# Two products of a chunked recurrence split into two halves of 64 channels

## The chip, the cores and the metric

The kernel runs on one core of a Trainium2 chip. A core has a matrix engine (TensorE, PE in the profile, with its weight loads listed as PEld), a vector engine (DVE), a scalar engine (ACT), GpSimd (POOL) and a queue engine (SP) that here starts all the DMAs. The metric is the device time of one execution in microseconds. Three runs of the kernel before took 1005.9, 1007.14 and 1010.24 us: the median is 1007.14 us.

## What is computed

The input x is 16 sequences of 128 tokens with 512 channels. A first layer is an RWKV block: layer norm, five mixed projections (k, w, v, r, g), a linear recurrence over the tokens in 32 heads of 16 channels, a group norm, a gate, an output projection and a gated feed-forward. A second layer is an attention of x over a context. The part that matters here is the recurrence. For each head, with a state s of 16 by 16:

```python
def step(s, rkvw):
    r_t, k_t, v_t, w_t = rkvw
    a = k_t[..., :, None] * v_t[..., None, :]
    out = jnp.einsum('bhi,bhij->bhj', r_t, u * a + s)
    s = a + w_t[..., :, None] * s
    return (s, out)
```

Written out, the output of token t is the sum over earlier tokens s of the scalar "r_t times all decays between times k_s" times v_s, plus a term with u for s = t, plus r_t times the decayed starting state.

## The kernel before

All arithmetic is float32. The 16 sequences are worked in 8 groups g of n = 2 sequences b. Each group passes through stages: stageB and stageB2 (norm, mixing, projections), stageR (the recurrence), stageC (output projection and feed-forward), stageL (attention), with stageE and stageX making and loading the context's tensors. A step of the outer loop holds different stages of different groups (OFF, ORDER, DLY); `interleave` advances them piece by piece, at their `yield`s, and so several independent streams of work lie in each engine's program at the same time. The order of the instructions in each engine's queue is then chosen by the framework's own scheduler, which places an instruction when its inputs and its buffer are expected to be ready. On the chip, every engine takes its queue in that order.

Channels lie on partitions in stageR: 512 channels are 4 blocks `cc` of 128 partitions, each block 8 heads of 16 channels. The 128 tokens are cut into 4 chunks c of 32. Three products on TensorE belong together:

- The level products (L433 to L453). Inside a chunk, pairs of tokens at distances of 4, 8 and 16 are done level by level (LEV). A copy of k, `ks`, is spread by 8 DMAs into `KX` (`expand`, L402 to L410): for each block KX has 8 slots, one for each head, and head h fills only its own 16 partitions of slot h; all else stays zero from the start. A product of r (32 tokens of one chunk as weights, 128 channels deep) with KX (16 tokens for 8 heads, 128 columns) gives the pair values of all 8 heads at once, since the zeros keep the heads apart (L441). The four chunks write four different groups of 32 partitions of one PSUM bank `pl`, one bank for each sequence. Then `copy_predicated` on DVE moves the valid ones into `AM` (L445).
- The states at chunk starts (L468 to L504). `pu` holds the products of k and v of a chunk (L489): weights of 32 tokens by 64 channels, so two chunks (different rows of TensorE) and two halves of the channels (different columns) take four parts of the array; chunk 2 is done by itself. DVE decays the state of each chunk (`Sn`, L497), adds `pu` (L498), and `spread` (L474) writes it with zeros between the heads (mask `bdm`) into `Sx`, 8 slots of 16 columns for each chunk and block.
- The output `po` (L513 to L524). For each block, four products of r (128 channels deep) with Sx (L517, 128 columns), and eight products of the transposed AM with v (L522, 64 columns) that add to the same PSUM bank. ACT copies `po` to `y` (L526).

PSUM buffers are taken in turn by tag. `pq`, `p4`, `pl`, `pk`, `pu`, `pa` and `po` all share the tag "lv", which has two banks: each new one waits until the last but one is read out.

A float32 matmul in this kernel shows as two weight loads and two matmul instructions; a transpose as one of each. The profile writes a matmul's place as rows*columns of the array: `128*32` is 128 rows by 32 columns, `32*64` is 32 rows by 64 columns.

Of the kernel before, what the change touches and what calls it, by code (L numbers as in the profile page):

```python
# [7 lines left out]
FP = mybir.dt.float32  # L8
# [3 lines left out]
ALU = mybir.AluOpType  # L12
# [6 lines left out]
n = 2  # L19
# [15 lines left out]
def rwkv_xattn_kernel(ctx: ExitStack, tc: tile.TileContext, a: dict, out: bass.AP):  # L35
    nc = tc.nc
    const = ctx.enter_context(tc.tile_pool(name="const", bufs=1))
    small = ctx.enter_context(tc.tile_pool(name="small", bufs=4))
    ps = ctx.enter_context(tc.tile_pool(name="ps", bufs=1, space=bass.MemoryType.PSUM))
    dr = ctx.enter_context(tc.tile_pool(name="dr", bufs=2, space=bass.MemoryType.DRAM))  # L40
    sb = ctx.enter_context(tc.tile_pool(name="sb", bufs=2))
    sb1 = ctx.enter_context(tc.tile_pool(name="sb1", bufs=1))
# [31 lines left out]
    st = load("st", [128, 2, 4, B])  # L74
    w1 = load("maa_w1", [128, 4, 160])

    LATE = dict(td_w1=[128, 4, 64], td_w2=[128, 512], l1w=[128, 4, 128], l1b=[128, 4], emat=[128, 32], bdm=[128, 8, 16],
                lvm=[128, 3, 16], dgm=[128, 32])
    late = {k: const.tile(v, I32 if k in ("lvm", "dgm") else FP, name=k) for k, v in LATE.items()}
    td1, td2, l1w, l1b, emat, bdm, lvm, dgm = late.values()  # L80
# [20 lines left out]
    stk = [const.tile([98, 5, 256], FPR, name=f"sk{i}") for i in range(2)]  # L101


    KX = const.tile([128, 4 * n, 8, 64], FP, name="KX")
# [248 lines left out]
    def stageR(g):  # L353
        d = D[g]
        k, r, w, vt = d["k"], d["r"], d["w"], d["vt"]

        wl = sb1.tile([128, 4 * n, 124], FP, name="wl")
        src = w.rearrange("p c b t -> p (c b) t")
        for m in PRO:
# [42 lines left out]
        def expand(li):  # L402

            m = LEV[li]
            ks = sb1.tile([128, 4 * n, 64], FP, name="ks", tag="sq")
            nc.scalar.copy(ks.rearrange("p a (q m) -> p a q m", m=m),
                           kf.rearrange("p a (q s m) -> p a q s m", s=2, m=m)[:, :, :, 0])
            for h in range(8):
                p = slice(16 * h, 16 * h + 16)
                nc.sync.dma_start(out=KX[p, :, h], in_=ks[p])  # L410

        def wblock(m, half):
            if m == 1:
# [17 lines left out]
        decay(rf, 2, 1)  # L431
        yield
        for li, m in enumerate(LEV):  # L433
            pl = []
            for b in range(n):
                t = ps.tile([128, 512], FP, name="pl", **T("lv"))
                pl.append(t)
                for cc in range(4):
                    for c in range(4):
                        cs = slice(32 * c, 32 * c + 32)  # L440
                        nc.tensor.matmul(t[cs, 128 * cc : 128 * cc + 128], lhsT=r[:, cc, b, cs],  # L441
                                         rhs=KX[:, n * cc + b, :, 16 * c : 16 * c + 16], start=True, stop=True)
            yield
            for b in range(n):
                nc.vector.copy_predicated(  # L445
                    AM[:, b].rearrange("p h (q s m) -> p h q s m", s=2, m=m)[:, :, :, 0],
                    lvm[:, li].rearrange("p (q m) -> p q m", m=m)[:, None].to_broadcast([128, 32, 16 // m, m]),
                    pl[b].rearrange("p (h q m) -> p h q m", h=32, m=m))
            decay(rf, m, 1)
            if li < 2:  # L450
                expand(li + 1)
                decay(kf, 2 * m, 0)
            yield  # L453
        y = sb1.tile([128, n, 512], FP, name="y")
        var = small.tile([128, n, 32], FP, name="var", bufs=2)
        for b in range(n):

            for q in range(4):
                nc.sync.dma_start(out=VX[32 * q : 32 * q + 32, :, q],
                                  in_=d["vD"][:, b, 128 * q : 128 * q + 128].rearrange("(c s) f -> s c f", s=32))  # L460
# [7 lines left out]
            Sx = sb1.tile([128, 4, 4, 8, 16], FP, name="Sx")  # L468
            Sc = s0[:, b, :, None, :].to_broadcast([128, 4, 4, 16])

            def spread(c, src):

                o = Sx[:, c].rearrange("p m (a q) j -> p m a (q j)", a=2)
                nc.vector.tensor_tensor(o, src, bdm.rearrange("p (a q) j -> p a (q j)", a=2)[:, None].to_broadcast([128, 4, 2, 64]), ALU.mult)  # L474

            nc.vector.tensor_tensor(Sx[:, 0], s0[:, b, :, None, :].to_broadcast([128, 4, 8, 16]),
                                    bdm[:, None].to_broadcast([128, 4, 8, 16]), ALU.mult)
            vb = vt[:, b].rearrange("p (q x j) -> p x q j", q=4, x=8)
            yield

            pu = [ps.tile([128, 4, 4, 16], FP, name="pu", **T("lv")) for _ in range(2)]

            def gains(cs_):
                for cc in range(4):
                    for hf in range(2):
                        f = slice(64 * hf, 64 * hf + 64)
                        for c in cs_:
                            cs = slice(32 * c, 32 * c + 32)
                            nc.tensor.matmul(pu[c][f, cc], lhsT=kt[cs, 128 * cc + 64 * hf : 128 * cc + 64 * hf + 64],  # L489
                                             rhs=vb[cs, 2 * cc + hf], start=True, stop=True)  # L490

            gains((0, 1))
            yield
            for c in range(3):
                wc = wl.rearrange("p (c b) s -> p c b s", b=n)[:, :, b, WOFF[32] + c]
                Sn = sb.tile([128, 4, 4, 16], FP, name="Sn")
                nc.vector.tensor_tensor(Sn, Sc, wc[:, :, None, None].to_broadcast([128, 4, 4, 16]), ALU.mult)  # L497
                nc.vector.tensor_tensor(Sn, Sn, pu[c], ALU.add)  # L498
# [4 lines left out]
                Sc = Sn  # L503
                yield  # L504

            at = sb1.tile([128, 8, 128], FP, name="at")
            for x4 in range(2):
                pa = ps.tile([128, 4, 128], FP, name="pa", **T("lv"))
                for x in range(4):
                    nc.tensor.transpose(pa[:, x], AM[:, b, 4 * (4 * x4 + x) : 4 * (4 * x4 + x) + 4].rearrange("p h s -> p (h s)"), ident)  # L510
                nc.scalar.copy(at[:, 4 * x4 : 4 * x4 + 4], pa)
            yield
            po = ps.tile([128, 512], FP, name="po", **T("lv"))  # L513
            for cc in range(4):
                for c in range(4):
                    cs = slice(32 * c, 32 * c + 32)
                    nc.tensor.matmul(po[cs, 128 * cc : 128 * cc + 128], lhsT=r[:, cc, b, cs],  # L517
                                     rhs=Sx[:, c, cc].rearrange("p h j -> p (h j)"), start=True, stop=True)
                for x in (2 * cc, 2 * cc + 1):
                    for c in range(4):  # L520
                        cs = slice(32 * c, 32 * c + 32)
                        nc.tensor.matmul(po[cs, 64 * x : 64 * x + 64], lhsT=at[:, x, cs],  # L522
                                         rhs=VX[:, c, :, 16 * x : 16 * x + 16], start=False, stop=True,
                                         skip_group_check=True)  # L524
            yield
            nc.scalar.copy(y[:, b], po)  # L526
# [226 lines left out]
def _prep(np, inp):  # L753

    f = lambda nm: np.asarray(inp[nm])
# [12 lines left out]
    r = {}  # L768
# [18 lines left out]
    s0 = ctx[:, 2:18].reshape(G, n, 4, 8, 16, 16)  # L787
# [6 lines left out]
    r["bdm"] = np.repeat(r["emat"][:, 0:8, None], 16, 2)  # L794
    t = p % 32
    q = np.arange(16)
    lv = []
    for m in LEV:
        s = q // m * 2 * m + q % m
# [23 lines left out]
```

## Time and profile before

| | |
|---|---|
| median of three runs | 1007.14 us |
| the profiled execution's own time | 1012.07 us |
| its span from first to last instruction | 1010.3 us |
| mean granted clock of TensorE | 0.973 |
| TensorE busy | 919.9 us (91%) |
| DVE busy | 648.3 us (64%) |
| ACT busy | 495.6 us (49%) |
| level products (L441) | 1536 instructions, busy 52.3 us |
| state products (L517) | 512 instructions, busy 29.0 us |

Busy time is the time in which at least one instruction of the group was under way, so instructions that overlap count once. A mean duration is that of one instruction from start to modelled end; where four instructions run at the same time in four parts of the array, the group's time is far below their number times the mean. The chain of waits is the list of work, followed back from the last instruction, that sets the end; its pieces follow one another in time without overlap, so the time of a piece of TensorE work divided by its instructions says how fast the engine got through them. The 40 slices show the busy share over the span, 25 us each.

### The profile page before, as it was taken

The page shows a single profiled execution, that of the slowest core. Times are in us where ns is not written, and L with a number is a line of the kernel's source. Part 1 is how long each engine was busy: PE and PEld are TensorE (multiplying, and loading weights), DVE is VectorE, ACT ScalarE, POOL GpSimd, SP SyncE. Part 2 cuts the span into 40 slices and gives each one's busy share as a digit, 9 for nine tenths or more (in the row PEclk, how much of TensorE's full clock was granted, in tenths as well). Part 3 has the DMA queues.
Part 4 walks back from the last instruction along what each step waited for, and adds up shares of the span by engine and source line. Part 5 has one row for each costly group of instructions (what it writes and reads, how often), then busy time and mean ns, then how long its engine had stood idle before and what let it go on. Part 6 is the DMA issues. An engine that isn't in the chain of part 4 may idle for free.

```text
span 1010.3 us, 19691 instructions
## 1 busy us (share of the span) xinstructions
PE 919.9 (91%) x7780; PEld 632.1 (63%) x7780; DVE 648.3 (64%) x1609; ACT 495.6 (49%) x1049; POOL 60.3 (6%) x92
## 2 busy tenths in 40 slices
PE   3799999898999899999989999999999997997965
PEld 2576867565566776586757666676757555754643
DVE  7767787874694778667945785597746754543231
ACT  3555273353343754644545553365535454546343
POOL 6201010000000000000000000000000000000000
PEclk9799999999899999999999999999999998999997
DMA  6755647357324245453345334624344433333200
GB/s 169 237 188 181 198 162 255 82 160 217 100 63 127 88 136 153 132 182 112 95 108 176 108 101 118 178 77 158 84 120 155 144 80 91 95 94 94 83 22 21
DMA packets 76461, 129.93 MB, mean 129 GB/s; under 512 B 33697, under 2 KB 43425, under 8 KB 76368
## 3 DMA queue, kind: packets, MB, share of 16 engines
q1 hardware_dynamic: 76370, 128.68, 42.1%
q8 instruction: 61, 1.00, 0.4%
q14 instruction: 30, 0.25, 0.1%
HBM read 100.32 MB, written 22.04 MB: 121 GB/s over the span
## 4 chain that ended last, share of the span: by engine, by line
PE 67%; DVE 11%; DMA 10%; ACT 7%; SPq 2%; issue 2%; POOL 0%; DVEq 0%; ACTq 0%; POOLq 0%
PE ptk L576 16%; PE pj L219 11%; PE pj L603 5%; PE pv L326 5%; PE pO L702 5%; PE pS L688 4%; PE pl L441 4%; PE pA L697 2%; DMA out_dram<-x 2%; SPq L410 2%; PE po L517 1%; PE po L522 1%; PE p L240 1%; PE pu L489 1%; DMA x<-in_x_dram 1%
## 5 line engine op out<-in xcount | busy, mean ns | idle before, releaser
L219 PE MATMUL pj<-xm,wb 128*128 128x256 f32 x768 | 181.5, 387 | 7.0 <-DMA wb<-in_Wk_dram 3.5
L219 PEld LDWEIGHTS pj<-xm,wb 128*128 128x128 f32 x768 | 143.9, 193 | 37.6 <-issue 8.5
L138 POOL TENSOR_TENSOR rs<-rs,mhalf 128x1 f32<-128x1 f32 x64 | 43.1, 680 | 752.9 <-DVE rs L123 681.8
L702 PEld LDWEIGHTS pO<-AT,MV 128*128 128x128 f32 x448 | 59.1, 198 | 22.3 <-ACT AT L699 10.3
L692 ACT ACTIVATE e<-pS,nm 128x512 f32<-128x512 f32 x64 | 44.4, 695 | 52.6 <-DVE nm L690 52.6
L702 PE MATMUL pO<-AT,MV 128*128 128x128 f32 x448 | 63.6, 286 | 6.3 <-ACT AT L699 6.3
L690 DVE TENSOR_REDUCE nm<-pS 128x1 f32<-128x512 f32 x64 | 43.7, 687 | 38.6 <-PE pS L688 38.6
L688 PE MATMUL pS<-MV,Mn 128*128 128x512 f32 x112 | 60.6, 624 | 6.6 <-DMA MV<-mvD 5.5
L576 PE MATMUL ptk<-wb,kk 128*128 128x512 f32 x128 | 60.5, 617 | 5.8 <-DMA wb<-in_Wfv_dram 5.7
L286 DVE TENSOR_TENSOR xm<-px,sx 128x512 f32<-128x512 f32 x80 | 53.9, 685 | 18.2 <-PE px L283 18.0
L694 ACT ACTIVATE e<-e,nm 128x512 f32<-128x512 f32 x64 | 46.1, 726 | 33.4 <-DVE nm L693 33.3
L699 ACT COPY AT<-pA 128x512 f32<-128x512 f32 x64 | 37.6, 587 | 48.9 <-PE pA L697 43.3
L576 PE MATMUL ptk<-wb,sx 128*128 128x512 f32 x128 | 58.4, 598 | 1.1 <-DMA wb<-in_Wfr_dram 1.1
L326 PE MATMUL pv<-wb,xm 128*128 128x512 f32 x128 | 58.6, 603 | 0.6 <-DVE xm L286 0.6
L603 PE MATMUL pj<-xk,wb 128*128 128x256 f32 x256 | 58.4, 382 | 0.2 <-DVE xk L145 0.2
L576 PE MATMUL ptk<-wb,yT 128*128 128x512 f32 x128 | 58.0, 602 | 0.0
L703 DVE SCALAR_TENSOR_TENSOR x<-pO,cb,x 128x128 f32<-128x128 f32 x64 | 22.2, 348 | 51.5 <-PE pO L702 51.3
L441 PE MATMUL pl<-KX,r 128*32 128x128 f32 x1536 | 52.3, 275 | 2.6 <-DMA KX<-ks 2.6
L287 DVE TENSOR_TENSOR xm<-xm,xaT 128x512 f32<-128x512 f32 x80 | 54.2, 684 | 0.3
L603 PEld LDWEIGHTS pj<-xk,wb 128*128 128x128 f32 x256 | 47.5, 190 | 7.8 <-ACT AT L699 0.8
L697 PE MATMUL pA<-ident,e 128*128 128x128 f32 x256 | 41.8, 288 | 11.3 <-ACT e L694 9.7
L697 PEld LDWEIGHTS pA<-ident,e 128*128 128x128 f32 x256 | 30.7, 146 | 33.4 <-ACT e L694 16.1
(162 smaller groups left out, 1684.2 us busy)
## 6 DMA issues: line engine op xcount, KB each, us to landing
mvD<-MVe SPq DMA_DIRECT2D x16, 512.0 KB, 5.3
wb<-in_Wk_dram SPq DMA_DIRECT2D x16, 512.0 KB, 3.8
wb<-in_Wr_dram SPq DMA_DIRECT2D x16, 512.0 KB, 3.7
wb<-wvc SPq DMA_DIRECT2D x16, 512.0 KB, 3.5
wb<-in_Wg_dram SPq DMA_DIRECT2D x16, 512.0 KB, 4.7
wb<-in_Wo_dram SPq DMA_DIRECT2D x16, 512.0 KB, 3.6
wb<-in_Wfk_dram SPq DMA_DIRECT2D x16, 512.0 KB, 4.2
wb<-in_Wfr_dram SPq DMA_DIRECT2D x16, 512.0 KB, 3.7
```

The lines of the kernel that those rows point to most:

```text
L219: nc.tensor.matmul(pj[:, m], lhsT=wb[:, m, cc, :], rhs=xm[:, cc], start=cc == 0, stop=cc == 3)
L286: nc.vector.tensor_tensor(xm[:, sl], px.rearrange("p c (b t) -> p c b t", b=n), sx[:, sl], ALU.mult)
L287: nc.vector.tensor_tensor(xm[:, sl], xm[:, sl], xaT[:, sl, :, 1:129], ALU.add)
L326: nc.tensor.matmul(pv, lhsT=xm[:, m, b], rhs=wbs[m // 2][:, m % 2], start=m == 0, stop=m == 3)
L441: nc.tensor.matmul(t[cs, 128 * cc : 128 * cc + 128], lhsT=r[:, cc, b, cs], rhs=KX[:, n * cc + b, :, 16 * c : 16 * c + 16], start=True, sto ...
L576: nc.tensor.matmul(pt, lhsT=act[:, m, b], rhs=wbs[m // 2][:, m % 2], start=m == 0, stop=m == 3)
L603: nc.tensor.matmul(pj[:, m], lhsT=wb[:, m, cc, :], rhs=xk2[:, cc], start=cc == 0, stop=cc == 3)
L688: nc.tensor.matmul(pS, lhsT=Mn[:, tsl], rhs=Mm, start=True, stop=True)
L692: nc.scalar.activation(e, pS, AF.Exp, bias=nm[:, 0:1], accum_out=nm[:, 1:2])
L694: nc.scalar.activation(e, e, AF.Identity, scale=nm[:, 2:3])
L697: nc.tensor.transpose(pA[:, sc], e[:, 128 * sc : 128 * sc + 128], ident)
L702: nc.tensor.matmul(pO, lhsT=Vc[:, sc], rhs=AT[:, sc], start=sc == 0, stop=sc == 3)
```

## The change

The level products and the state products are made in two halves x of 64 channels (4 heads) each. KX, Sx and the mask bdm get 4 slots instead of 8; heads h and h + 4 share a slot, on different partitions. Each product becomes two, with 64 rows of TensorE and 64 columns of output each. The two halves lie in different rows of the array, and each has a PSUM bank of its own: `pl` is one bank for each half (with both sequences in it) instead of one for each sequence, and `po` is two banks instead of one. `copy_predicated` works half by half. `spread` is gone: the state is kept in the masked form all along, so `pu` is masked first, and then Sx of the next chunk is the decayed Sx plus that. The copy of po to y becomes two copies. The products of AM and v (L522) stay as they are, but write the bank of their half.

```diff
-                for cc in range(4):
-                    for c in range(4):
                         cs = slice(32 * c, 32 * c + 32)
-                        nc.tensor.matmul(t[cs, 128 * cc : 128 * cc + 128], lhsT=r[:, cc, b, cs],
-                                         rhs=KX[:, n * cc + b, :, 16 * c : 16 * c + 16], start=True, stop=True)
+                        for x in range(2):
+                            f = slice(64 * x, 64 * x + 64)
+                            nc.tensor.matmul(pl[x][cs, b, cc], lhsT=r[f, cc, b, cs],
+                                             rhs=KX[f, n * cc + b, :, 16 * c : 16 * c + 16], start=True, stop=True)
...
-            for b in range(n):
+            for x in range(2):
                 nc.vector.copy_predicated(
...
-                nc.vector.tensor_tensor(Sn, Sc, wc[:, :, None, None].to_broadcast([128, 4, 4, 16]), ALU.mult)
-                nc.vector.tensor_tensor(Sn, Sn, pu[c], ALU.add)
+                nc.vector.tensor_tensor(Sn, pu[c], own, ALU.mult)
+                nc.vector.tensor_tensor(Sx[:, c + 1], Sx[:, c], wc[:, :, None, None].to_broadcast([128, 4, 4, 16]), ALU.mult)
+                nc.vector.tensor_tensor(Sx[:, c + 1], Sx[:, c + 1], Sn, ALU.add)
...
-                spread(c + 1, Sn.rearrange("p m q j -> p m (q j)")[:, :, None].to_broadcast([128, 4, 2, 64]))
...
-            po = ps.tile([128, 512], FP, name="po", **T("lv"))
+            po = [ps.tile([128, 4, 64], FP, name="po", **T("lv")) for _ in range(2)]
             for cc in range(4):
                 for c in range(4):
                     cs = slice(32 * c, 32 * c + 32)
-                    nc.tensor.matmul(po[cs, 128 * cc : 128 * cc + 128], lhsT=r[:, cc, b, cs],
-                                     rhs=Sx[:, c, cc].rearrange("p h j -> p (h j)"), start=True, stop=True)
-                for x in (2 * cc, 2 * cc + 1):
+                    for x in range(2):
+                        f = slice(64 * x, 64 * x + 64)
+                        nc.tensor.matmul(po[x][cs, cc], lhsT=r[f, cc, b, cs],
+                                         rhs=Sx[f, c, cc].rearrange("p h j -> p (h j)"), start=True, stop=True)
+                for x in range(2):
...
-            nc.scalar.copy(y[:, b], po)
+            for x in range(2):
+                nc.scalar.copy(y[:, b].rearrange("p (c x f) -> p c x f", x=2, f=64)[:, :, x], po[x])
```

More of the change, by code (lines that the diff above doesn't have):

```diff
@@ L75, in rwkv_xattn_kernel @@
     w1 = load("maa_w1", [128, 4, 160])
-    LATE = dict(td_w1=[128, 4, 64], td_w2=[128, 512], l1w=[128, 4, 128], l1b=[128, 4], emat=[128, 32], bdm=[128, 8, 16],
+    LATE = dict(td_w1=[128, 4, 64], td_w2=[128, 512], l1w=[128, 4, 128], l1b=[128, 4], emat=[128, 32], bdm=[128, 4, 16],
                 lvm=[128, 3, 16], dgm=[128, 32])
@@ L101, in rwkv_xattn_kernel @@
     stk = [const.tile([98, 5, 256], FPR, name=f"sk{i}") for i in range(2)]
-    KX = const.tile([128, 4 * n, 8, 64], FP, name="KX")
+    KX = const.tile([128, 4 * n, 4, 64], FP, name="KX")
     VX = const.tile([128, 4, 4, 128], FP, name="VX")
@@ L409, in expand @@
                 p = slice(16 * h, 16 * h + 16)
-                nc.sync.dma_start(out=KX[p, :, h], in_=ks[p])
+                nc.sync.dma_start(out=KX[p, :, h % 4], in_=ks[p])
         def wblock(m, half):
@@ L433, in stageR @@
         for li, m in enumerate(LEV):
-            pl = []
+            pl = [ps.tile([128, n, 4, 64], FP, name="pl", **T("lv")) for _ in range(2)]
             for b in range(n):
-                t = ps.tile([128, 512], FP, name="pl", **T("lv"))
-                pl.append(t)
                 for cc in range(4):
@@ L440, in stageR @@
                         cs = slice(32 * c, 32 * c + 32)
[L441 to L442 removed]
+                        for x in range(2):
+                            f = slice(64 * x, 64 * x + 64)
+                            nc.tensor.matmul(pl[x][cs, b, cc], lhsT=r[f, cc, b, cs],
+                                             rhs=KX[f, n * cc + b, :, 16 * c : 16 * c + 16], start=True, stop=True)
             yield
[L444 removed]
+            for x in range(2):
                 nc.vector.copy_predicated(
[L446 to L448 removed]
+                    AM.rearrange("p b (c x h) (q s m) -> p (b c) x h q s m", x=2, h=4, s=2, m=m)[:, :, x, :, :, 0],
+                    lvm[:, li].rearrange("p (q m) -> p q m", m=m)[:, None, None].to_broadcast([128, 4 * n, 4, 16 // m, m]),
+                    pl[x].rearrange("p b c (h q m) -> p (b c) h q m", h=4, m=m))
             decay(rf, m, 1)
@@ L466, in stageR @@
             nc.scalar.copy(kt, pk)
[L468 to L477, printed above, removed]
+            Sx = sb1.tile([128, 4, 4, 4, 16], FP, name="Sx")
+            own = bdm[:, None].to_broadcast([128, 4, 4, 16])
+            nc.vector.tensor_tensor(Sx[:, 0], s0[:, b, :, None, :].to_broadcast([128, 4, 4, 16]), own, ALU.mult)
             vb = vt[:, b].rearrange("p (q x j) -> p x q j", q=4, x=8)
@@ L501, in stageR @@
                     gains((2,))
-                spread(c + 1, Sn.rearrange("p m q j -> p m (q j)")[:, :, None].to_broadcast([128, 4, 2, 64]))
-                Sc = Sn
                 yield
@@ L516, in stageR @@
                     cs = slice(32 * c, 32 * c + 32)
-                    nc.tensor.matmul(po[cs, 128 * cc : 128 * cc + 128], lhsT=r[:, cc, b, cs],
-                                     rhs=Sx[:, c, cc].rearrange("p h j -> p (h j)"), start=True, stop=True)
-                for x in (2 * cc, 2 * cc + 1):
+                    for x in range(2):
[3 more added lines that the diff above has]
+                for x in range(2):
                     for c in range(4):
                         cs = slice(32 * c, 32 * c + 32)
-                        nc.tensor.matmul(po[cs, 64 * x : 64 * x + 64], lhsT=at[:, x, cs],
-                                         rhs=VX[:, c, :, 16 * x : 16 * x + 16], start=False, stop=True,
+                        nc.tensor.matmul(po[x][cs, cc], lhsT=at[:, 2 * cc + x, cs],
+                                         rhs=VX[:, c, :, 16 * (2 * cc + x) : 16 * (2 * cc + x) + 16], start=False, stop=True,
                                          skip_group_check=True)
             yield
-            nc.scalar.copy(y[:, b], po)
+            for x in range(2):
+                nc.scalar.copy(y[:, b].rearrange("p (c x f) -> p c x f", x=2, f=64)[:, :, x], po[x])
             sq = sb1.tile([128, 512], FP, name="sq")
@@ L793, in _prep @@
     r["emat"] = (p[:, None] // 16 == np.arange(32)).astype(np.float32)
-    r["bdm"] = np.repeat(r["emat"][:, 0:8, None], 16, 2)
+    r["bdm"] = np.repeat((p[:, None] // 16 % 4 == np.arange(4)).astype(np.float32)[:, :, None], 16, 2)
     t = p % 32
```

## The prediction

> **What bounds the kernel now.** I read the page's first two parts, then the chain of waits by engine, then the groups of TensorE, and last the chain in order of time around the three products that change.
>
> ```profile
> PE 919.9 (91%) x7780; PEld 632.1 (63%) x7780; DVE 648.3 (64%) x1609; ACT 495.6 (49%) x1049; POOL 60.3 (6%) x92
> ...
> PE   3799999898999899999989999999999997997965
> ...
> PE 67%; DVE 11%; DMA 10%; ACT 7%; SPq 2%; issue 2%; POOL 0%; DVEq 0%; ACTq 0%; POOLq 0%
> ```
>
> TensorE is busy nearly all the time from 75 us to 900 us (slices 4 to 36), and it carries 67% of the chain that sets the end. The changed products start between 105 and 881 us, so they all lie where TensorE is the bound. DVE carries 11%, though it is busy 64%.
>
> ```profile
> L441 PE MATMUL pl<-KX,r 128*32 128x128 f32 x1536 | 52.3, 275 | 2.6 <-DMA KX<-ks 2.6
> L517 PE MATMUL po<-Sx,r 128*32 128x128 f32 x512 | 29.0, 283 | 0.0
> L522 PE MATMUL po<-VX,at 128*32 128x64 f32 x1024 | 28.2, 224 | 0.0
> L474 DVE TENSOR_TENSOR Sx<-Sn,bdm 128x512 f32<-128x512 f32 x48 | 33.0, 687 | 0.7
> L498 DVE TENSOR_TENSOR Sn<-Sn,pu 128x256 f32<-128x256 f32 x48 | 19.9, 415 | 5.7 <-PE pu L489 5.1
> L476 DVE TENSOR_TENSOR Sx<-s,bdm 128x512 f32<-128x512 f32 x16 | 11.0, 688 | 23.6 <-PE po L517 23.6
> L526 ACT COPY y<-po 128x512 f32<-128x512 f32 x16 | 9.3, 583 | 21.8 <-PE po L522 21.8
> L376 ACT ACTIVATE ru<-r,vec 128x256 f32<-128x256 f32 x32 | 13.7, 501 | 0.0
> ```
>
> These are the groups that the change touches: three of TensorE, whose instructions wait for almost nothing; then what DVE and ACT do around them. The last line is only a row for a copy of 256 columns.
>
> ```profile
> 195.13 1.09 PE pw L304 x14
> ...
> 207.12 1.75 PE pl L441 x64
> 208.86 0.33 PE p L244 x24
> ...
> 216.50 1.89 PE pl L441 x64
> ...
> 226.11 0.62 PE pu L489 x32
> ...
> 232.11 0.61 PE pu L489 x16
> ```
>
> This is the chain in order of time (start, us, work). [...]
>
> **Price 1, a round.** 64 level instructions take 1.75 us where the neighbours have the same 128*32 shape (L244 after it): 16 rounds of four, one for each group of 32 columns, at 109 ns for 128 columns. With 64 columns, 24 instructions of L244 take 0.33 us: 6 rounds of four at about 56 ns. So a round costs what its columns cost, and half the columns is half the time.
>
> **Price 2, different rows.** L489 does two chunks at once in 0.62 us (32 instructions in two groups of rows), and one chunk alone in 0.61 us (16). A second group of rows with its own bank is free. L304 agrees for 64 rows: 14 instructions that alternate between the row halves in 1.09 us, 78 ns each, though a round of 128 columns takes 109. I therefore take a round of eight (four column groups by two halves) at 57 ns, where the halves alternate in the queue. The bound above is that four more instructions must be started: 114 ns, no gain from rows.
>
> **Price 3, a change of shape.** The same 64 level instructions take 1.89 us where the work before them was a full 128*128 matmul (L326). The border costs 0.14 us. The records show it as about 95 ns more than the last matmul needs to stream, at every border between shapes (128*128, 128*64, 128*32, 64*128, 32*64), then a first round some 25 ns longer for 32 columns. I take 0.12 us; 0.14 is the upper bound. The new 64*32 shape stands beside 128*32 (L522) in `po`; this pair is not in the trace. Other borders that change only the rows are: L304 (64*128) followed by full matmuls, which pay the same. So I take 0.12 there too; the lower bound is nothing.
>
> [...]
>
> **What the change does to the queue.** The text of the loop alternates x, but the scheduler orders the queue. The instruction order of the changed kernel can be read before it runs. KX for heads 0 to 3 is loaded by the first four DMAs, the bank of half 0 in `po` comes free with the first copy of `pa`, and so the scheduler places runs of half 0 and then runs of half 1. Of the 1536 matmuls of `pl`, 574 alternate in pairs of halves and 962 stand in runs of one half; of the 512 state products, 198 alternate and 314 don't. In most `po` the order is four of half 0, four of AM and v, four of half 0, and so on. Changes of shape along the whole queue rise from 290 to 494: between state products and AM-v products there were none, and now there are 168 inside `po`; the rest is level products split by other streams' work.
>
> **The sum, on TensorE.**
> - Level products before: 1536 / 4 = 384 rounds at 109 ns, 41.9 us. After: 962 x 2 / 4 = 481 rounds of four and 574 x 2 / 8 = 143.5 of eight, at 57 ns: 35.6 us. Gain 6.3 us, of the 20 us that full alternation would give. Overlap where a run of half 0 meets one of half 1 could add up to 4 us; the 64 rows of L304 show a little of it, and I take 1 us.
> - State products before: 128 rounds at 109 ns, 14.0 us. After: 157 rounds of four and 49.5 of eight, 11.8 us. Gain 2.2 us.
> - L522 stays: 1024 instructions, 64 columns.
> - Changes of shape: 204 x 0.12 = 24.5 us lost (28.6 by 0.14).
>
> TensorE thus gets 15 us more (24.5 less 9.5). By lines, the chain has 37.8 us of L441 and 27.6 of L517 and L522, which is some nine tenths of their rounds; the drains that are added lie in the same place, in front of matmuls that wait for nothing. At 0.9, that is +13.5 us.
>
> **The sum, elsewhere.** DVE: `spread` (687) becomes an operation of 256 elements (415): 48 x 0.27 = 13.1 us less; L476 loses 16 x 0.27 = 4.4. Per chunk there are still three operations, in the same order behind `pu`. 17.4 us less on an engine with 64% busy and 11% of the chain: 17.4 x 11 / 64 = -3 us (bounds 0 and -9: L474, L476, L497 and L498 whole, as far as they are on the chain). `copy_predicated` moves the same 512 elements 48 times, at 713: nothing, hidden or not. ACT: two copies of 256 columns at 403 (the cast L258) to 501 (L376) for one at 583: 16 x 0.2 to 0.4 = 3.6 to 6.7 us more on an engine with 7% of the chain, +0.5 to +1. Bank turns: `po` takes both "lv" banks, so its half 1 waits for the second copy of `pa` (581 ns), and the next `pk` waits for `po`'s first copy. Other streams' matmuls lie between in the queue; without that cover it is 0.5 us in each of 16 `po`, 8 us; I take +1. The DMAs into KX keep number and size, and SP's queue its order of work; half 0 may start before the last four have landed, which is worth at most half of a level's 1.75 us at the 4 places where the chain holds a KX landing: -1. The clear of KX on POOL and the load of `bdm` are smaller, at the start, behind other loads: nothing.
>
> Sum: 13.5 - 3 + 0.7 + 1 - 1 = +11 us. The profiled execution took 1012.07 us (span 1010.3), 5 above the median; added to it the sum gives 1023, and to the median 1007.14 it gives **1018 us**.
>
> **Rivals.**
> 1. *No drain between 64*32 and 128*32* (same columns, only rows regrouped). Then 170 of the 494 borders are free: 324 against 290, 4 us lost. TensorE -5.4, the rest -2.5: 1000 us, faster. For it: no border of just this pair in the trace. Against: every pair in the trace pays, row-only pairs too. It decides as soon as such a border costs under 0.05 us.
> 2. *Eight at once does not work*: alternating rounds take 114 ns. 143.5 + 49.5 rounds x 57 = 11 us more, x 0.9: 1028 us. For it: eight starts must fit into 57 ns. Against: L489, L304.
> 3. *The drains are covered*: in the stretches where the chain runs through DVE, DMA or ACT (a third of the span), TensorE has slack; if half of the 15 us vanishes there, with DVE's 3 us gained, 1011 us, within what can be told. For it: chain 67%. Against: L517 and L522 waited 0.0 us.
> 4. *The scheduler's new order* costs or saves at stages that the change does not touch; several us either way, in no row; it widens each case.
>
> **How the numbers follow.** My forecast 0.62, rival 1 0.12, rival 2 0.12, rival 3 0.14. About 0.5% (5 us) is what a measurement of this kernel can tell from no change. Forecast alone: 1009 to 1026 (the drain at 0.10 to 0.14, DVE at 0 to -9, order). The range reaches to rival 1 and beyond rival 2: 1001 to 1031. Faster: rival 1 and a little of rival 3, 0.14. Same (1002 to 1012): rival 3 and the low end of mine, 0.20. Slower: 0.66.
>
> **What would show it.** Right: `pl` at 64*32 with 3072 instructions; 64 of them in one half about 0.9 us in the chain, alternating ones about half that; the lines of `po` together (L517 and L522 before) longer, not shorter, in pieces of four with a gap of 0.1 us between; DVE busy near 631; TensorE busy in slices as before. Wrong: no gaps inside `po` (rival 1), alternating runs no faster than single ones (rival 2), or a chain that moves from TensorE to DVE or to a bank of "lv" (rival 3).

## The result, and the profile after

The changed kernel took 1044.43 us, the median of four runs (1043.36 to 1046.77); the kernel before took 1008.69 in the same series. The ratio is 1.035, with a 95% interval of 1.029 to 1.040. The forecast was 1018 us in a range of 1001 to 1031: the sign was right, the loss was three times as large, and it lies outside the range.

The page of the changed kernel, with lines of its first, third and fourth parts (busy time by engine; the queue that loads instructions: packets, MB, share; the chain that ended last), then the groups of the changed lines, with idle time and what ended it in the last column:

```profile
PE 941.8 (90%) x9828; PEld 638.5 (61%) x9828; DVE 632.9 (61%) x1609; ACT 497.1 (48%) x1065; POOL 60.7 (6%) x92
...
q8 instruction: 77, 1.26, 0.5%
...
PE 65%; DVE 12%; DMA 9%; ACT 6%; SPq 3%; issue 3%; POOL 0%; ACTq 0%; DVEq 0%; POOLq 0%
```

```profile
L442 PE MATMUL pl<-KX,r 64*32 64x64 f32 x3072 | 51.8, 221 | 14.3 <-DMA KX<-ks 7.6 <-issue 6.2 <-DVE r L421 0.5
...
L512 PE MATMUL po<-Sx,r 64*32 64x64 f32 x1024 | 34.4, 228 | 0.1
L517 PE MATMUL po<-VX,at 128*32 128x64 f32 x1024 | 33.6, 227 | 0.0
L446 DVE COPY_PREDICATED AM<-lvm,pl 128x512 f32<-128x512 int32 x48 | 32.3, 703 | 21.0 <-PE pl L442 20.9
```

DVE is 15.4 us less busy (17.4 in the forecast), and the time goes up all the same. The level products are hardly cheaper (51.8 us for 52.3), and TensorE now sits idle 14.3 us in front of them, where it was 2.6. The two lines of `po` together are busy 68.0 us instead of 57.2. The chain has the shape it had, TensorE first; no other engine has become the bound.

The chain in order of time (start, us, what) shows two of the causes. First a `po` that is made in pieces of one shape and then the other:

```profile
148.13 0.25 PE po L512 x8
148.38 0.25 PE po L517 x8
148.63 0.25 PE po L512 x8
148.88 0.25 PE po L517 x8
149.12 0.25 PE po L512 x8
...
151.69 0.36 PE po L517 x16
152.05 0.27 PE po L512 x16
152.32 0.36 PE po L517 x16
```

Eight instructions of one half (two rounds of four) take 0.25 us, though sixteen of both halves (line at 152.05) take 0.27. Eight should take 0.11 by the row of L244 in the kernel before; the rest is the border in front of them. In the records of single instructions, nearly every border costs 90 to 97 ns more than the columns need, and the pair 64*32 and 128*32, which the trace of before does not have, costs 93 in one direction and 96 in the other.

Second, gaps inside the level products and elsewhere in which nothing is waited for:

```profile
112.62 2.12 DMA KX<-ks
114.74 0.14 issue
114.88 1.27 PE pl L442 x75
116.15 3.41 issue
119.56 0.45 PE pl L442 x10
...
319.08 0.23 PE p L244 x3
319.31 2.60 issue
321.90 0.48 PE p L244 x11
```

"issue" is time in which the engine waited for nothing that the profile shows. In the first gap only one thing moves that belongs to no tensor, a load on the queue for instructions (DMA in the window from 116 to 120 us):

```profile
q1 hardware_dynamic: 50, 0.14, 8.7%
q8 instruction: 1, 0.02, 2.2%
```

It is a packet of 16 KB that begins at 116.7 us. There are five such gaps of 1.6 to 3.6 us (near 120, 220, 322, 429 and 654 us), and in each TensorE resumes 2.2 to 2.9 us after a load of that kind began. TensorE's program has 2048 more matmuls, and the loads of code rise from 61, in this line of the page before, to 77:

```profile
q8 instruction: 61, 1.00, 0.4%
```

All 77 are of 16 KB, as are the 61 of before. That these gaps are waits for code is read from the timing alone.

**Where TensorE's time went.** I summed, over TensorE's queue, the time from each start to the next. Whatever exceeds what the columns need and 95 ns at a change of shape by over 0.17 us is "wait"; "drain" is my name for the number of borders times 95 ns; "work" is the rest. So "drain" is a count times the price that the records show. Time in which TensorE ran at half its clock (0.5 in the profile; 512 columns then take 853 ns from start to start for 429, see the last section) lies in "work" for small products, and for products of 256 columns and more in "wait": by the clock of the profile some 12 us of the waits of before and 15 of after are of that kind.

| us | before | after | difference |
|---|---|---|---|
| work | 864.5 | 862.5 | -2.0 |
| drain (290 and 494 borders) | 27.5 | 46.9 | +19.4 |
| wait | 106.8 | 120.9 | +14.1: 11.5 in the five gaps, 5.0 more on loads of KX, -2.4 elsewhere |
| sum | 998.8 | 1030.3 | +31.5 |

The spans of the two profiled executions differ by 31.3 us (the medians by 35.7; the profiled execution of before was 3.4 us above its median). So the table accounts for it: some 17 us of TensorE's own, near what was forecast, and 14 us of waits, which were not. What made the waits is the question for the experiments.

### The profile page after: what moved, and what is told of

The parts are those of the page before. It is cut to its first block, busy times and chain, and to the rows that moved or that the text cites. A ratio compares the mean times of both kernels' runs of the same rounds, so it can differ in the third digit from the quotient of the medians.

```text
span 1041.6 us, 23780 instructions
## 1 busy us (share of the span) xinstructions
PE 941.8 (90%) x9828; PEld 638.5 (61%) x9828; DVE 632.9 (61%) x1609; ACT 497.1 (48%) x1065; POOL 60.7 (6%) x92
## 4 chain that ended last, share of the span: by engine, by line
PE 65%; DVE 12%; DMA 9%; ACT 6%; SPq 3%; issue 3%; POOL 0%; ACTq 0%; DVEq 0%; POOLq 0%
PE ptk L572 13%; PE pj L219 12%; PE pO L698 5%; PE pj L599 5%; PE pv L326 4%; PE pS L684 4%; PE pl L442 3%; SPq L410 3%; PE po L517 2%; PE po L512 2%; PE pA L693 2%; DMA KX<-ks 2%; DVE PP L379 2%; DMA out_dram<-x 1%; DVE xm L286 1%
## 5 line engine op out<-in xcount | busy, mean ns | idle before, releaser
L219 PE MATMUL pj<-xm,wb 128*128 128x256 f32 x768 | 184.2, 392 | 7.2 <-DMA wb<-in_Wk_dram 4.0
L219 PEld LDWEIGHTS pj<-xm,wb 128*128 128x128 f32 x768 | 146.0, 196 | 36.3 <-DVE xm L287 5.0
L138 POOL TENSOR_TENSOR rs<-rs,mhalf 128x1 f32<-128x1 f32 x64 | 46.6, 734 | 788.6 <-DVE rs L123 698.4
L286 DVE TENSOR_TENSOR xm<-px,sx 128x512 f32<-128x512 f32 x80 | 54.1, 685 | 28.0 <-PE px L283 27.8
L698 PEld LDWEIGHTS pO<-AT,MV 128*128 128x128 f32 x448 | 56.7, 192 | 22.2 <-ACT AT L695 11.9
L442 PE MATMUL pl<-KX,r 64*32 64x64 f32 x3072 | 51.8, 221 | 14.3 <-DMA KX<-ks 7.6
L442 PEld LDWEIGHTS pl<-KX,r 64*32 64x32 f32 x3072 | 42.2, 106 | 30.9 <-issue 24.1
L693 PE MATMUL pA<-ident,e 128*128 128x128 f32 x256 | 41.9, 288 | 11.3 <-ACT e L690 9.4
```

What stands on the lines that cost most here:

```text
L138: D["pow"] = nc.gpsimd.tensor_tensor(rs, rs, mhalf[:, 0:1], ALU.pow).ins
L219: nc.tensor.matmul(pj[:, m], lhsT=wb[:, m, cc, :], rhs=xm[:, cc], start=cc == 0, stop=cc == 3)
L286: nc.vector.tensor_tensor(xm[:, sl], px.rearrange("p c (b t) -> p c b t", b=n), sx[:, sl], ALU.mult)
L442: nc.tensor.matmul(pl[x][cs, b, cc], lhsT=r[f, cc, b, cs], rhs=KX[f, n * cc + b, :, 16 * c : 16 * c + 16], start=True, stop=True)
L693: nc.tensor.transpose(pA[:, sc], e[:, 128 * sc : 128 * sc + 128], ident)
L698: nc.tensor.matmul(pO, lhsT=Vc[:, sc], rhs=AT[:, sc], start=sc == 0, stop=sc == 3)
```

## The experiments

All times are medians; the kernel before ran beside each group, at 1010.9 to 1011.4 us (after is compared with its own series, 1008.7). "In the order of before" means that after the kernel is built, each instruction gets the place that its counterpart has in the queue of the kernel before, and order-only dependencies chain each engine's queue in that sequence:

```diff
+    for queue in lines.values():
+        queue.sort(key=lambda q: q[:2])
+        for before, after in zip(queue, queue[1:]):
+            tc.add_manual_dep(after[2], before[2].name, nosync, reason="pin")
```

The kernel before with these dependencies alone was not run; level_apart_pinned below (0.995) says that they cost little.

| kernel | us | ratio, 95% | borders | work, drain, wait (us) |
|---|---|---|---|---|
| before, beside the groups | 1011 | 1 | 290 | 864.5, 27.5, 106.8 |
| after | 1044.4 | 1.035 [1.029, 1.040] | 494 | 862.5, 46.9, 120.9 |
| level_alone | 1044.9 | 1.032 [1.027, 1.037] | 314 | 861.9, 29.8, 139.2 |
| state_alone | 1052.5 | 1.041 [1.038, 1.044] | 440 | 869.4, 41.8, 129.4 |
| level_columns | 1045.4 | 1.034 [1.031, 1.038] | 330 | 877.2, 31.3, 122.4 |
| state_grouped | 1066.2 | 1.055 [1.051, 1.059] | 366 | 871.0, 34.8, 147.4 |
| level_columns_pinned | 1015.1 | 1.005 [1.002, 1.007] | 290 | 868.0, 27.5, 106.2 |
| after_pinned | 1046.6 | 1.035 [1.032, 1.039] | 401 | 863.2, 38.1, 130.7 |
| level_alone_pinned | 1025.9 | 1.016 [1.012, 1.020] | 293 | 856.4, 27.8, 127.0 |
| state_alone_pinned | 1031.2 | 1.020 [1.017, 1.023] | 398 | 867.6, 37.8, 111.6 |
| level_apart_pinned | 1008.0 | 0.995 [0.993, 0.997] | 293 | 865.2, 27.8, 103.4 |
| level_mixed_pinned | 1005.1 | 0.992 [0.989, 0.995] | 293 | 855.3, 27.8, 107.6 |
| state_turns_pinned | 1022.3 | 1.010 [1.006, 1.013] | 338 | 874.6, 32.1, 106.8 |
| after_turns_pinned | 1021.4 | 1.010 [1.007, 1.013] | 341 | 867.9, 32.4, 103.9 |
| after_mixed_pinned | 1020.2 | 1.008 [1.005, 1.011] | 341 | 861.1, 32.4, 109.8 |
| null_c | 1021.3 | 1.010 [1.007, 1.014] | 271 | 865.0, 25.7, 114.8 |
| null_po | 1034.6 | 1.022 [1.019, 1.025] | 282 | 870.6, 26.8, 124.9 |
| null_pu | 1021.9 | 1.010 [1.008, 1.012] | 297 | 863.6, 28.2, 116.7 |

### First theory: borders and loads of code

The theory was that the loss is the sum of what the trace of after shows: drains by their number, and the gaps. The rivals put it into one of the two parts. One part at a time, then the borders alone:

level_alone: the level part of the change, the state part as before.

```diff
+            pl = [ps.tile([128, n, 4, 64], FP, name="pl", **T("lv")) for _ in range(2)]
...
+                        for x in range(2):
+                            f = slice(64 * x, 64 * x + 64)
+                            nc.tensor.matmul(pl[x][cs, b, cc], lhsT=r[f, cc, b, cs],
```

> Only the level products in two halves; the state products as in the kernel before. 314 borders between shapes against 290 before, 630 of 1536 level matmuls alternate. Theory (borders at 0.12 us, plus a new cost: TensorE's code arrives too slowly where 64-column instructions stand dense): rounds -6 us, borders +3 us, code stalls about +10 us, so 1013 to 1020 us, and waits of 1.5 us or more inside the level products that no semaphore ends. Rival (the scheduler's other order makes TensorE wait for the loads of KX, no code stall): waits in front of runs of the level products that end with a KX landing, 1005 to 1012 us.

state_alone: the other part, with the level products as before.

```diff
+            po = [ps.tile([128, 4, 64], FP, name="po", **T("lv")) for _ in range(2)]
...
+                    for x in range(2):
+                        f = slice(64 * x, 64 * x + 64)
+                        nc.tensor.matmul(po[x][cs, cc], lhsT=r[f, cc, b, cs],
```

> Only the state products in two halves (Sx masked, po in two banks); the level products as before. 440 borders against 290, 164 of them inside po; 236 of 512 state matmuls alternate. Theory: borders 150 x 0.12 = +18 us, rounds -2 us, DVE 0 to -3 us, no code stalls: 1020 to 1025 us, TensorE's drains +14 us in the records. Rival (the two lv banks that po takes make TensorE wait): the same time or more, but as waits in front of po and pk, with drains short of +14 us.

level_columns: as many instructions as level_alone, but no halves of rows; each product of 128 columns is only cut into two of 64.

```diff
-                        nc.tensor.matmul(t[cs, 128 * cc : 128 * cc + 128], lhsT=r[:, cc, b, cs],
-                                         rhs=KX[:, n * cc + b, :, 16 * c : 16 * c + 16], start=True, stop=True)
+                        for x in range(2):
+                            nc.tensor.matmul(t[cs, 128 * cc + 64 * x : 128 * cc + 64 * x + 64], lhsT=r[:, cc, b, cs],
+                                             rhs=KX[:, n * cc + b, 4 * x : 4 * x + 4, 16 * c : 16 * c + 16], start=True, stop=True)
```

> The kernel before with each level product cut into two of 64 columns, but still 128 rows deep: 3072 instructions of the 128*32 shape, no halves of rows, no second bank, no change on DVE. 768 rounds of 57 ns against 384 of 109: +2 us; 330 borders against 290: +5 us. Theory (code arrives too slowly): here 64 instructions still take 0.9 us as in the changed kernel's single runs, so stalls of about 10 us in all, 1020 to 1026 us. Rival (order and KX loads): no more than the +7 us, 1012 to 1016 us.

state_grouped: the whole change, with the state products of all four blocks ahead of the AM-v products. All state products keep their start flag. A part of the computation is left out by it: its output is off by 0.038 (relative). Which part was not measured; the instructions are the same.

```diff
+            for cc in range(4):
                 for x in range(2):
                     for c in range(4):
                         cs = slice(32 * c, 32 * c + 32)
                         nc.tensor.matmul(po[x][cs, cc], lhsT=at[:, 2 * cc + x, cs],
```

> The changed kernel with the 32 state matmuls of po all written ahead of its 32 AM-v matmuls. 366 borders against 494, 30 inside po against 168. Theory: 128 x 0.12 = -15 us against the changed kernel, 1028 to 1031 us; code stalls stay. Rival (the waits for the two banks of po are the loss, or the drains were covered): within 5 us of the changed kernel's 1044 us.

All four missed, at 1044.9, 1052.5, 1045.4 and 1066.2 us. Each part alone costs as much as the whole, so the losses do not add. level_alone has only 24 borders more than before and 2.9 us of gaps without a semaphore, and loses 3.2% (of its 32 us of added waits, some 12 are products at half clock); state_grouped has fewer borders than after and loses more. The drains and gaps are in the records, but the theory that they sum to the loss fell. What the four have in common is that the scheduler made a new order of everything. In level_columns even the numbers of rows and banks are those of before.

### Second theory: the scheduler's new order

Here the same edits run in the order of before. level_columns_pinned is level_columns with that and nothing else:

> The column cut again, but every engine's queue is held in the order of the kernel before (each cut matmul's two parts stand where the one stood); 290 borders, as before. Theory now (the 30 us come from the scheduler's new order of all the work, not from the edit): rounds +2 us and a few us of code stalls, 1009 to 1018 us. Rival (dense 64-column instructions cost the time themselves): still above 1035 us.

after_pinned is the whole change; the two halves of each product stand side by side where the one product stood, so every pair alternates:

> The changed kernel with every queue held in the order of the kernel before; the two halves of a product then stand side by side, so all 1536 and 512 matmuls alternate; 401 borders, 108 of them inside po. Theory (order): level rounds 41.9 to 21.9 us, state rounds 14 to 7.3 us, borders 111 x 0.12 = +13 us, DVE 0 to -3 us: -14 to -17 us, so 992 to 1002 us with some code stalls. Rival (the halves, their banks or the code stalls make the loss): above 1030 us. If rounds of eight do not work, 1022 us or so.

level_alone_pinned and state_alone_pinned are the two parts in the same way:

> The level products alone in halves, queues held in the order of before, 293 borders, all 1536 alternate. Theory (order): rounds 41.9 to 21.9 us and nothing against it but code stalls: 990 to 1000 us. Rival (the halves themselves): near the 1045 us of the unpinned one.

> The state products alone in halves, queues held in the order of before, 398 borders, all 512 alternate. Theory (order): borders 108 x 0.12 = +13 us, rounds -6.7 us, DVE 0 to -3 us: 1010 to 1018 us. Rival (po's two lv banks): above 1035 us, with waits in front of po or pk.

level_columns falls from 1045.4 to 1015.1 us when only its order is put back. Some 30 us of its loss were order and nothing else. The other three were expected near or below the time before, and missed: 1046.6, 1025.9 and 1031.2. So the whole change loses as much in the order of before, with its halves side by side, as in the scheduler's. The three have in common what level_columns_pinned has not: halves of rows, and two banks that are both needed at the first pair. The groups of the two parts show TensorE and DVE waiting at the banks. level_alone_pinned:

```profile
L442 PE MATMUL pl<-KX,r 64*32 64x64 f32 x3072 | 43.2, 230 | 11.4 <-issue 9.4 <-DVE AM L397 1.3 <-DMA KX<-ks 0.6
...
L446 DVE COPY_PREDICATED AM<-lvm,pl 128x512 f32<-128x512 int32 x48 | 32.7, 705 | 42.6 <-PE pl L442 42.6
```

and the second line in before:

```profile
L445 DVE COPY_PREDICATED AM<-lvm,pl 128x512 f32<-128x512 int32 x48 | 33.8, 713 | 18.1 <-PE pl L441 17.1
```

state_alone_pinned:

```profile
L511 PE MATMUL po<-Sx,r 64*32 64x64 f32 x1024 | 27.2, 237 | 9.0 <-ACT at L503 8.9
...
L464 PE MATMUL pk<-ident,k 128*128 128x128 f32 x64 | 10.6, 291 | 3.4 <-ACT y L521 3.4
```

The level products themselves are cheap now (43.2 us for 52.3). But TensorE waits in front of them, mostly without a releaser that the profile shows. In the records of six of the eight groups, the gap of 1.5 to 2.7 us lies behind the first matmul of the first level, that is, at the first product of half 1, whose bank `p4` has held; in the chain at 196 us TensorE goes on 0.09 us after DVE has read it (L397). And DVE waits 42.6 us for the level products where it waited 17.1 before: 26.1 us of that stand in front of the first copies of the first levels (0.7 before, and 6.4 for the second copies), since half 0 is made in step with half 1, which has to wait for its bank. In state_alone_pinned the second bank of `po` comes free with the second copy of `pa` (L503), and `pk` behind it waits for the copies of `po` (L521). By the sums over starts, its waits in front of `po` and `pk` grow by 10.7 and 4.1 us against before.

### Third theory: both banks at the first product

If that is it, the loss goes when the halves are made one after the other, so that the second bank is needed later, as in the kernel before. level_apart_pinned: all of half 0 of a level, then all of half 1, in the places of the two sequences. In words:

```diff
-pl: (half 0, half 1) of product 1, of product 2, ... of product 32
+pl: half 0 of products 1 to 32, then half 1 of products 1 to 32
```

> Level products in halves, queues held in the order of before, but all of half 0 stands where sequence 0 stood and all of half 1 where sequence 1 stood: nothing alternates, the second bank is needed only half-way. Theory (the pinned loss of 15 us comes from needing both lv banks at the first matmul): 768 rounds of 57 ns are 43.8 us, +2 us, and the waits in front of pl fall back to before's: 1010 to 1017 us. Rival (half-depth products, or their two copies on DVE, cost the time): 1022 us or more.

level_mixed_pinned: the first level of each group apart, because there `p4` still holds the second bank; levels 2 and 3 alternating.

> Level products in halves, queues held in the order of before; the first level of each group apart (there the second bank is held by p4's reading), levels two and three alternating. Theory (the bank wait is at the first level, 1.6 us in 8 groups): rounds of eight at the measured 77 ns save 8 us of TensorE and the waits stay low: 1000 to 1011 us. Rival (both copies on DVE now start only when the whole level is done): 1015 to 1024 us, with the chain on the copies of AM.

state_turns_pinned: the state part alone; in the queue each `po` has all state products of half 0, then the AM-v products of half 0, then the same of half 1, so that there are three changes of shape inside a `po`, 48 in all. Only the first block's products set the start flag, and nothing is lost:

```diff
-                                         rhs=Sx[f, c, cc].rearrange("p h j -> p (h j)"), start=True, stop=True)
+                                         rhs=Sx[f, c, cc].rearrange("p h j -> p (h j)"), start=cc == 0, stop=True,
+                                         skip_group_check=cc > 0)
+            for cc in range(4):
```

> State products in halves, queues held in the order of before; in each po first all of half 0 (state products, then AM-v), then all of half 1, so its second bank is needed only half-way; 338 borders, 48 of them inside po, against 398 and 108 in the alternating pinned one. Theory (both banks at once cost 15 us there, borders the rest): borders 48 x 0.12 = +6 us, rounds 0, DVE 0 to -3 us: 1012 to 1018 us. Rival (masking on DVE or the extra copies on ACT cost it): 1025 us or more.

after_turns_pinned: both parts, every level apart, `po` as in state_turns_pinned.

> The changed kernel with both of these orders; 341 borders. Theory: the sum of the two, 1014 to 1024 us, against 1046 us for the alternating pinned one. Rival: 1035 us or more.

The level part goes from 1025.9 to 1008.0 us with the halves apart (2 us below the expected range) and to 1005.1 when they alternate only where the bank is free. The halves of rows stay in both, so they were not the loss. The latter kernel is faster than the one before, by 0.8% (0.5 to 1.1). Its groups:

```profile
L442 PE MATMUL pl<-KX,r 64*32 64x64 f32 x3072 | 44.4, 223 | 0.0
...
L446 DVE COPY_PREDICATED AM<-lvm,pl 128x512 f32<-128x512 int32 x48 | 32.7, 704 | 21.4 <-PE pl L442 21.0
```

Against level_alone_pinned, TensorE no longer waits in front of `pl`, and DVE waits 21.4 us instead of 42.6; the products are as cheap. The chain of the same kernel shows what an alternating level is worth (the chain counts 91 of a level's 128 instructions; the records have all 128):

```profile
303.87 1.42 PE pl L442 x91
305.29 1.02 PE py L563 x8
...
317.09 1.42 PE pl L442 x91
```

of level_apart_pinned:

```profile
306.62 1.93 PE pl L442 x128
...
320.36 1.93 PE pl L442 x128
```

and of before:

```profile
307.75 1.89 PE pl L441 x64
...
321.44 1.89 PE pl L441 x64
```

1.42 us for 1.93, and 1.89 before, at the same two levels. Without the border, the alternating level is some 1.23 us, 16 rounds of eight at 77 ns. The halves work in parallel, but not at the 57 ns that I had taken from rows with fewer parts. The 77 is an average: in the records of the undisturbed alternating levels the second and third rounds take 56 ns each, the fifth 147, and the others 66 to 103. What slows the later rounds was not tested.

For the state part, turns brought it from 1031.2 to 1022.3, between the expected range and its rival. The waits in front of `po` are down to 2.5 us over before, but 1% is left. By the sums over starts, 4.6 us of it is drain, and 10 is work. Its profiled execution took 1026.7 us, 4.4 above its median, so the sums show more than the median has. In it TensorE ran at half its clock for some 80 us in all, and for 57 in before: 23 us at half rate add some 11. Why this kernel is there for longer was not found, and the 1% is not explained. after_turns_pinned came out as expected, at 1021.4; by -0.5% and +1.0% of the parts it should have been nearer to +0.5 than to its +1.0%.

### Does a new order cost anything by itself?

The second theory was shown for a kernel with cut products only. Three edits change no instruction at all, only the sequence in which a loop of the source issues them. null_c:

```diff
-                    for c in range(4):
+                    for c in (3, 2, 1, 0):
```

> The kernel before with one edit that changes no instruction: the loop over the four chunks c of the level products counts down (3, 2, 1, 0). Same instructions, same shapes, same banks; the scheduler gives another order (of the 697 runs of one tile in TensorE's queue, 437 stand in the same sequence as before). Theory 'order': any new order costs what the column cut costs, 15 to 45 us: 1020 to 1055 us, ratio 1.015 to 1.045, and the cost shows as waits of TensorE, not as work or drain. Rival 'the order is only bad where the products are cut small': within 0.7% of before, 1004 to 1018 us.

null_po:

```diff
-            for cc in range(4):
+            for cc in (3, 2, 1, 0):
```

> The kernel before with another edit that changes no instruction: the loop over the four blocks cc in the output po counts down. The scheduler's order differs more (319 of 697 runs in the same sequence; the changed kernel has 308). Theory 'order': 1020 to 1055 us. Rival: 1004 to 1018 us.

null_pu:

```diff
-                    for hf in range(2):
+                    for hf in (1, 0):
```

> The kernel before with a third edit of that kind: in pu the upper half of the channels is made before the lower (460 of 697 runs in the same sequence). Theory 'order': 1015 to 1055 us. Rival: 1004 to 1018 us. With the other two it shows how far orders of the same work scatter.

They took 1021.3, 1034.6 and 1021.9 us: 1.0, 2.2 and 1.0% more than before, for the same 7780 matmuls. The rival (within 0.7%) falls. The theory holds for the sign and for null_po's size; null_c, at 10 us, costs less than the 15 us that the theory gave as its least, though its time is inside the range. Their waits are 8 to 18 us longer than before and their drains within 2 us; null_po has 6 us more of work as well. No single wait makes null_po's loss (waits of TensorE: us in total, times, longest):

```profile
PE pO L702 <- ACT AT L699: 10.0, 16, 1.5
PE pt L200 <- DMA w<-in_maa_w_dram: 9.1, 1, 9.1
...
PE pq L390 <- DVE PP L379: 3.9, 2, 2.8
PE pA L697 <- DVE gt L538: 3.3, 1, 3.3
...
PE pl L441 <- DVE sk L257: 2.7, 1, 2.7
```

The 9.1 us stand in front of TensorE's very first instruction, where before has 7.7. The table by stretches (start:end; length; busy of PE, PEld, DVE, ACT, POOL with instructions; clock; DMA share; GB/s) shows null_po behind in one stretch, with a lower clock, and working off the rest at the end:

```profile
200.00:400.00 200.00, 183.08 (x1654) 126.37 (x1653) 125.07 (x309) 86.56 (x189) 8.58 (x14) 0.92 0.39 116
400.00:600.00 200.00, 193.97 (x1695) 133.85 (x1694) 141.58 (x341) 102.75 (x224) 8.64 (x16) 1.00 0.42 126
...
800.00:1000.00 200.00, 176.37 (x1374) 110.43 (x1373) 96.75 (x257) 104.18 (x209) 8.38 (x12) 0.97 0.30 91
```

Before has in the first and the last of these stretches:

```profile
200.00:400.00 200.00, 189.51 (x1707) 131.74 (x1707) 138.65 (x339) 93.56 (x201) 9.09 (x15) 0.97 0.44 129
800.00:1000.00 200.00, 166.63 (x1130) 105.93 (x1129) 84.16 (x226) 97.02 (x197) 6.26 (x11) 0.95 0.25 75
```

after_mixed_pinned: the whole change in the order of before, the levels as in level_mixed_pinned and `po` as in state_turns_pinned. One thing in its expectation doesn't apply to it: inside a `po` there are three changes of shape, as in state_turns_pinned, not one. Its start flags are those of state_turns_pinned too, and nothing is lost.

> The whole change in the order of before: first level of each group all of half 0 and then half 1, second and third level alternating, and in po the state products of all blocks, then the AM-v products (one change of shape). From the runs so far: the level part so placed measured -0.8%, the state part by turns +1.0%, the whole by turns with all levels apart +1.0%. Theory 'the parts add': +0.2 to +1.0%, 1012 to 1022 us. Rival 'the level part's gain is lost beside the state part': +1.0 to +1.5%. [...]

1020.2 us, +0.8%, within the range given for "the parts add". But -0.8 and +1.0 would give +0.2, and the interval is 0.5 to 1.1, so they don't quite add. It has 77 loads of code as after has, but only 0.8 us of gaps like those: in another order as many loads cost next to nothing.

## Why the prediction was wrong, step by step

- **The sum on TensorE came out near**: +15 forecast, +17.4 in the table (work -2.0, drain +19.4). The counts of shapes and borders were read before the run and hold. In part it is luck. By the same records, without waits and borders, the starts inside `pl` take 41.9 us for 45.4, and those of `po` 35.2 for 31.2 (slower first rounds behind a border included). So the 9.5 us that the rounds were to gain came out as nothing, some 5 us of it, at 25 ns for each of 204 borders, because of those first rounds, which the forecast had in its 0.12; the -2.0 come from products that the change does not touch.
- **Price 3, a change of shape, was right**: 93 to 96 ns for the new pair too. Rival 1 (no drain there) is excluded.
- **Price 2, a round of eight at 57 ns, was mis-sized**: 77 ns on average in the alternating levels. With 143.5 + 49.5 such rounds it is 4 us too little. It also settles rival 2 (114 ns, no gain): it is excluded, the measured value lies between.
- **Eight starts in 57 ns, the doubt of rival 2**: they took 77 ns, 9.6 from start to start. The row of L244 in the kernel before has 14 (24 in 0.33 us).
- **Bank turns, "I take +1" with 8 as the bound, held for after and not for other orders.** In after the order has mostly runs of half 0 and then of half 1, and the waits in front of `po` and `pk` are 0.6 us by the sums over starts. In state_alone_pinned, where the halves alternate, they are 10.7 and 4.1 us, above the bound. Of the level part's banks I had said nothing; when their halves alternate throughout, the kernel takes 1025.9 - 1008.0 = 18 us more than with the halves apart.
- **DMAs into KX, -1, failed in sign**: the wait for them in front of `pl` grew from 2.6 to 7.6 us. Half 0 needs the first four loads only, but with the order of before the wait is 0.6 us in level_alone_pinned and 0.8 in after_pinned, so the rise belongs to the new order.
- **Loads of code were not in the prediction**: 11.5 us of gaps, if the timing is read rightly. They depend on the order too, since after_mixed_pinned has as many loads and 0.8 us of gaps.
- **Rival 4, the scheduler's new order, "several us either way", is the step that failed.** The sum of +11 has no term for it, and the range only a few us. Three edits without any new instruction cost 10, 23 and 11 us, all in the same direction, and the column cut 30 us that go away when the order is put back. I had the scheduler's order before the run and read only borders and alternation from it, not how far the rest had moved: only 308 of 697 runs of one tile stand in the sequence of before.
- DVE (632.9 busy for a forecast of 631), ACT and the copies of `po` went as forecast, and mattered little.

How the 35 us divide is not fully settled. The table has 17 of TensorE's own and 14 of waits. In the order of before, with the halves placed by hand so that banks are free and borders few, the change costs 9 to 10 us. The rest, some 25, is what the scheduler's order adds to that: it includes most of the added borders, since 494 become 341 there, and the waits. The comparison rests on that placing: in the order of before with the halves side by side (after_pinned) the loss is 35 us again, for the banks. Borders and order can't be taken apart further, because the order makes the borders.

## What to carry to other kernels

Where a scheduler orders the whole kernel, an edit can reorder all of it, and that alone made this kernel 1 to 2% slower in three edits, and 3% in the column cut; run an edit that changes no instruction first, to know that size, and test a change in the old order before judging it. When a product is split into halves with a bank each, make the halves one after the other until both banks are surely free, and alternate them only then (1005.1 us here, for 1025.9 with all of them alternating). Count changes of array shape, at 90 to 97 ns each in these traces: a small product between others of another shape can lose by the border what it gains by its size.

## What the runs showed of the hardware that was not expected

- **Eight parts of the array at once**: 77 ns on average for a round of 64 columns in eight parts, 9.6 ns per instruction (level_mixed_pinned), and about 56 in four (L244 in before, 0.33 us for six). The rounds are uneven, with the same pattern in each undisturbed level: 56 ns early, 66 to 147 later.
- **TensorE at half its clock, also in the middle of the work**: the clock that the profile records has windows of 3.4 to 13.7 us at 0.5. They add to 57 us in before, 66 in after, 80 in state_turns_pinned and 114 in state_grouped. In them a product of 512 columns takes 853 ns from start to start, and 429 outside (L576 in before). All 22 in before and after begin behind 3.4 us in which TensorE was busy for 0 to 58%; but after has such a stretch at 48% (922.9 to 926.3 us) with the full clock behind it. What triggers a window was not tested. If it is the idle time in front of it, a wait costs more here than its own length.
- **Gaps that look like waits for code**: in after TensorE stands still five times, for 1.6 to 3.6 us, without a sign but "issue" and a packet of 16 KB on the instruction queue that began 2.2 to 2.9 us before it goes on. That the packet is the cause was not tested.
- **Start flags and the output**: the output of state_grouped, whose state products all set the flag, is off by 0.038 (relative); that of state_turns_pinned, where only the first block's products set it, is that of the kernel before. The two differ in their order too, and the flag was not tested alone.
